# Last sequence's two experts: both first weights gathered before the second ones, the exp table loaded later, the second expert's part added to the sum from PSUM

## The chip, the cores and the metric

The kernel runs on one core of one Trainium2 chip. The metric is device microseconds (us) of one execution of the whole program. Engines are named as in the profile: PE does matrix products (PEld is its weight load), DVE is the vector engine, ACT the scalar engine with its function tables, POOL issues the indirect transfers, SP issues the plain ones. DVE and ACT read the matrix products out of PSUM, the accumulator memory[...]; everything else lies in SBUF.

## The reference, cut to what matters

Eight sequences of 1024 tokens with 256 channels pass a state-space layer (its recurrence over the tokens is the long part) with a feed-forward block, then attention with 8 heads, then a mixture of experts. The router looks at one sequence's mean, so all tokens of a sequence take the same two of the eight experts. In the reference this last part is

```python
logits = jnp.mean(x, axis=1) @ Wr + br                 # per sequence
...
top_w, top_i = jax.lax.top_k(rw_tok, K)                # K = 2
top_w = jax.nn.softmax(top_w, axis=-1)
h = jax.nn.gelu(jnp.einsum('nd,edf->enf', xf, W1) + b1[:, None, :], approximate=False)
y = jnp.einsum('enf,efd->end', h, W2) + b2[:, None, :]
out = jnp.einsum('ne,end->nd', w_dense, y).reshape(B, S, D)
out = _layer_norm(out + x, gamma, beta)
...
t = t + _L1_ffn_ref(_ln_t(t), ...)
```

So for each expert k of a sequence there are a product with W1 (256 to 512), a Gelu, a product with W2 (512 to 256), a weight w_k, and the sum of both; then the input is added, a layernorm follows, and the residual is added. The kernel centers W2 beforehand (the scratch tensor eW2_d), so the sum already has mean zero and the last layernorm needs only the variance.

## The kernel before, in words

Channels lie on partitions (256 channels are KC = 2 groups of 128), tokens along the free dimension, in chunks of CH = 512. A sequence is two chunks, c = 0 and 1. All data are fp32; the trace records two PE instructions for one fp32 product of 128 x 512.

The program is written as streams (Python generators: prologue, attention, experts, ...). Nothing schedules it afterwards: advance (L1808) walks a model clock, model.t, and lets each stream that is due emit its next instructions, the most urgent first. What a stream emits goes to the end of its engine's queue, and an engine takes its queue in order. A "yield" in a stream is a place where other streams may emit; "yield x" sets the model time from which the stream goes on. keep_warm (L1794) emits small products of 128 x 256 on zeros ("warm", or into a half bank under the name "halves") when the model sees PE free, so that PE stays busy.

All engine calls pass one helper, so nearly every instruction has the line L100 in the profile, and every transfer has L95; instructions are told apart by the names of what they write and read.

The part concerned is the end of the program. The last sequence (b = 7) has nothing after it, so it has its own path: experts (L1498) for b = B - 1 calls banks.widen(), which turns the two double PSUM banks that attention used into four single ones (named halves_0 and halves_1; names of tiles are shown without their numbers), so that six banks serve; then it starts two streams expert(b, 0, ...) and expert(b, 1, ...) (L1581) side by side. Each stream

- takes two SBUF tiles g1 and g2 and gathers its expert's weights by indirect DMA on the POOL queue: two gathers of 128 x 512 for W1 (L1587), at once followed by four of 128 x 256 for W2 (L1592). As the streams are started one after the other, the POOL queue holds g1, g2 of expert 0, then g1, g2 of expert 1;
- with k = 0 has weights() emit the small DVE work for the routing weights w2e and the two biases hbias and obias (L1482);
- for each chunk c: four products into PSUM (he, L1604), each taken out by ACT with a bias into the tiles he (names he<-halves,hbias and he<-he,hbias); two Gelus of 128 x 1024 on ACT (L1621); then lnexp() (L1623), which loads the table set with exp and ln; then two groups of four products (re, L1626), each taken out by ACT with weight w_k and bias into a tile r of this expert (L1634);
- when the second expert has its r for a chunk, finish_last (L1647) is started.

finish_last adds the two tiles r on DVE, adds the layernorm's input xf on DVE (two instructions of 128 x 1024), and runs layernorm (L387): ACT squares (sq_y), PE averages (16 short records), ACT does ln, exp and square on 128 x 128, DVE refines (two of 128 x 128), PE spreads the factors (pick), DVE scales, then adds beta and the residual t (four of 128 x 512), and SP writes the chunk out.

After both chunks, DVE forms a flag (L1950 to L1954), all engines load it and branch (L1957, L1960), and the program ends.

Of the kernel before, what the change touches and what calls it, by code (L numbers as in the profile page):

```python
# [12 lines left out]
AF = mybir.ActivationFunctionType  # L13
ALU = mybir.AluOpType
# [7 lines left out]
NCH = L // CH  # L22
# [32 lines left out]
def hybrid_kernel(ctx: ExitStack, tc: tile.TileContext, a: dict, out: bass.AP):  # L55
# [6 lines left out]
    class Model:  # L62
# [3 lines left out]
        t = end = moved = 0.0  # L66
# [10 lines left out]
    model = Model()  # L77
# [43 lines left out]
    def lnexp():  # L121

        act.preload_act_table_set("natural_log_exp_and_others")
# [146 lines left out]
    POLL = -1.0  # L270
# [204 lines left out]
    ends = {}  # L475
# [1022 lines left out]
    def experts(b: int):  # L1498

        rows1, rows2, w2e, hbias, obias, weights = yield from route(b)  # L1500
        if b == B - 1:

            banks.widen()
            parts = [[] for _ in range(NCH)]
            for k in range(2):
                start(
                    expert(b, k, rows1, rows2, w2e, hbias, obias, weights, parts), ("x", b, k),
                    model.t,
                )
            return  # L1510
        mem = Owner(t4, 5, 0)
        y_d = dram.tile([NCH, P, KC, CH], F32, name=f"y_d_{b}", tag="y_d", bufs=2)
        for k in range(2):
            g1 = yield from mem.take(f"g1_{b}_{k}")
            g2 = yield from mem.take(f"g2_{b}_{k}")
            g2v = g2.rearrange("p a (b n) -> p (a b) n", n=C)
            for i in range(KC):
                got = pool.indirect_dma_start(
                    out=g1[:, i, :], out_offset=None, in_=a["eW1"],
                    in_offset=bass.IndirectOffsetOnAxis(ap=rows1[:, k, i : i + 1], axis=0),  # L1520
                )
            for i in range(NF):
                pool.indirect_dma_start(
                    out=g2v[:, i, :], out_offset=None, in_=eW2_d,
                    in_offset=bass.IndirectOffsetOnAxis(ap=rows2[:, k, i : i + 1], axis=0),
                )
            if k == 0:
                yield
                weights()
            for c in range(NCH):  # L1530
                n = f"{b}_{k}_{c}"
                xf = yield from mem.take(f"xe_{n}")
                yield max(sp.dma_start(xf, xf_d[b][c]), got)
                hs, ps = [], None
                for f in range(NF + 1):
                    if f:
                        act.activation(
                            hs[(f - 1) // 2][:, 1 - f % 2, :], ps, AF.Identity,
                            bias=hbias[:, k, f - 1 : f],
                        )  # L1540
                        banks.put(ps)
                    if f < NF:
                        if f % 2 == 0:
                            hs.append((yield from mem.take(f"he_{n}_{f // 2}")))
                        ps = yield from banks.take(f"he_{n}_{f}")
                        for i in range(KC):
                            pe.matmul(
                                ps, g1[:, i, f * P : (f + 1) * P], xf[:, i, :],
                                start=(i == 0), stop=(i == KC - 1),
                            )  # L1550
                        yield
                mem.put(xf)
                for t in hs:
                    act.activation(t, t, AF.Gelu)
                lnexp()
                yield
                r = yield from mem.take(f"re_{n}")
                for m in range(KC):
                    ps = yield from banks.take(f"re_{n}_{m}")
                    for f in range(NF):  # L1560
                        pe.matmul(
                            ps, g2v[:, f, m * P : (m + 1) * P], hs[f // 2][:, f % 2, :],
                            start=(f == 0), stop=(f == NF - 1),
                        )
                    yield
                    act.activation(
                        r[:, m, :], ps, AF.Identity, bias=obias[:, k, m : m + 1],
                        scale=w2e[:, k : k + 1],
                    )
                    banks.put(ps)  # L1570
                yield
                mem.put(*hs)
                if k == 0:
                    mem.put(r, at=sp.dma_start(y_d[c], r))
                else:
                    mem.held -= 1
                    start(finish(b, c, r, y_d[c]), ("y", b, c), model.t)
            mem.put(g1, g2)
        mem.end()

    def expert(b: int, k: int, rows1, rows2, w2e, hbias, obias, weights, parts):  # L1581

        mem = Owner(t4, 5, 2)
        g1 = yield from mem.take(f"g1_{b}_{k}")
        g2 = yield from mem.take(f"g2_{b}_{k}")
        g2v = g2.rearrange("p a (b n) -> p (a b) n", n=C)
        for i in range(KC):  # L1587
            got = pool.indirect_dma_start(
                out=g1[:, i, :], out_offset=None, in_=a["eW1"],
                in_offset=bass.IndirectOffsetOnAxis(ap=rows1[:, k, i : i + 1], axis=0),  # L1590
            )
        for i in range(NF):  # L1592
            pool.indirect_dma_start(
                out=g2v[:, i, :], out_offset=None, in_=eW2_d,
                in_offset=bass.IndirectOffsetOnAxis(ap=rows2[:, k, i : i + 1], axis=0),
            )
        if k == 0:
            weights()
        yield got
        for c in range(NCH):  # L1600
            n = f"{b}_{k}_{c}"
            xf = ends[c][1]
            hs, ps = [], None
            for f in range(NF + 1):  # L1604
                if f:
                    act.activation(
                        hs[(f - 1) // 2][:, 1 - f % 2, :], ps, AF.Identity,
                        bias=hbias[:, k, f - 1 : f],
                    )
                    banks.put(ps)  # L1610
                if f < NF:
                    if f % 2 == 0:
                        hs.append((yield from mem.take(f"he_{n}_{f // 2}")))
                    ps = yield from banks.take(f"he_{n}_{f}")
                    for i in range(KC):
                        pe.matmul(
                            ps, g1[:, i, f * P : (f + 1) * P], xf[:, i, :],
                            start=(i == 0), stop=(i == KC - 1),
                        )
                    yield  # L1620
            for t in hs:  # L1621
                act.activation(t, t, AF.Gelu)
            lnexp()  # L1623
            yield
            r = yield from mem.take(f"re_{n}")
            for m in range(KC):  # L1626
                ps = yield from banks.take(f"re_{n}_{m}")
                for f in range(NF):
                    pe.matmul(
                        ps, g2v[:, f, m * P : (m + 1) * P], hs[f // 2][:, f % 2, :],  # L1630
                        start=(f == 0), stop=(f == NF - 1),
                    )
                yield
                act.activation(  # L1634
                    r[:, m, :], ps, AF.Identity, bias=obias[:, k, m : m + 1],
                    scale=w2e[:, k : k + 1],
                )
                banks.put(ps)
            yield
            mem.put(*hs)  # L1640
            parts[c].append(r)
            if len(parts[c]) == 2:
                start(finish_last(b, c, *parts[c], *ends[c]), ("y", b, c), model.t)
        mem.put(g1, g2)
        mem.end()

    def finish_last(b, c, r, r2, t, xf):  # L1647

        mem = Owner(t4, 4, 0, 4)
        vec.tensor_tensor(r, r, r2, ALU.add)  # L1650
        vec.tensor_tensor(r, r, xf, ALU.add)
        yield
        mem.put(r2, xf)
        yield from layernorm(mem, banks, r, r, f"y{b}_{c}", V("gamma"), centered=True)
        for m in range(KC):
            vec.scalar_tensor_tensor(
                r[:, m, :], r[:, m, :], V("beta", m), t[:, m, :], ALU.add, ALU.add
            )
        yield
        mem.put(t)  # L1660
        yield sp.dma_start(out_v[b, :, :, c * CH : (c + 1) * CH], r)
        mem.put(r)
        mem.end()
# [96 lines left out]
    with tc.tile_pool(name="work", bufs=1) as work_pool:  # L1760
# [30 lines left out]
        def start(stream, key, at=0.0):  # L1791
            due.append([at, URGENT[key[0]], len(done) + len(due), stream, key])
# [421 lines left out]
```

## Time and profile before

| what | us |
|---|---|
| median of 3 runs (lowest, highest) | 3543.58 (3540.22, 3544.69) |
| the profiled execution's own time | 3547.76 |
| its span, first to last instruction | 3546.0 |
| PE busy in the span | 3223.6 (91%) |
| DVE busy | 3070.7 (87%) |
| ACT busy | 2474.0 (70%) |
| first of the twelve gathers for b = 7 starts | 3443.71 |
| first product of the two experts starts | 3447.08 |
| last product of the two experts ends | 3522.88 |
| last chunk's store is issued | 3533.89 |

The profile gives for each instruction its start and duration in us from the start of the span, and in brackets how long its engine was idle before it and what ended that wait. An "x8" merges eight records of one kind that follow each other. In the records, ends of products are modelled: each overlaps the next by about 0.16 us. The stretch that the change touches is the last 100 us of a span of 3546 us. A wait for several semaphores is put down to the one that came last.

### The profile page before, as it was taken

To read this page: it belongs to the slowest core of one execution; us is meant where nothing else is said; L and a number is where in the kernel's file an instruction comes from. 1 tells how busy PE (TensorE), PEld (TensorE's weight loads), DVE (VectorE), ACT (ScalarE), POOL (GpSimd) and SP (SyncE) were. 2 spreads that over 40 slices of the span, in tenths; PEclk is the share of its full clock that TensorE was granted. 3 is DMA by queue.
4 is the path that set the end of the run, shared out by engine and by line. 5 is a ranking of instruction groups with operands and counts; after the bars stand their busy time and mean duration, and the time that the engine had idled before them with its cause. 6 is when DMAs were issued, how large, how long until landed. Compare 5 with 4: busy or idle time off the path is not lost. (4 is left out here: it accounts for less than half of the span.)

```text
span 3546.0 us, 39995 instructions
## 1 busy us (share of the span) xinstructions
PE 3223.6 (91%) x14425; PEld 1404.5 (40%) x14425; DVE 3070.7 (87%) x3160; ACT 2474.0 (70%) x3562; POOL 932.8 (26%) x1058
## 2 busy tenths in 40 slices
PE   8767878998999998989999999999999989999997
PEld 5454344333433344333433334333433343334344
DVE  6979999999999898999999899989998999942561
ACT  5643737785878776787778777886778777863644
POOL 0232223222331223323322233223422323211010
PEclk9878989999999999999999999999999999999999
DMA  4767888787888878898788988789888877842120
GB/s 124 191 133 162 193 184 187 171 199 181 196 204 186 187 182 191 187 202 200 181 195 191 201 188 192 180 188 215 197 203 191 196 174 183 211 110 72 36 75 16
DMA packets 189504, 607.79 MB, mean 171 GB/s; under 512 B 27056, under 2 KB 38000, under 8 KB 189296
## 3 DMA queue, kind: packets, MB, share of 16 engines
q0 software_dynamic: 103968, 366.54, 53.2%
q1 hardware_dynamic: 85328, 238.60, 20.9%
q8 instruction: 115, 1.88, 0.2%
q14 instruction: 93, 0.76, 0.1%
HBM read 238.58 MB, written 62.39 MB: 85 GB/s over the span
## 5 line engine op out<-in xcount | busy, mean ns | idle before, releaser
L100 ACT ACTIVATE da_all<-dt,vecs 128x512 f32<-128x512 f32 (+1 forms) x1024 | 702.3, 719 | 429.4 <-DVE hb L100 426.6
L95 POOL DMA_DIRECT2D dx<-hb x512 | 444.4, 870 | 1680.4 <-DVE hb L100 1334.3
L100 DVE TENSOR_TENSOR hb<-hb,bc 128x1024 f32<-128x1024 f32 x512 | 624.5, 1220 | 36.5 <-POOL state L100 26.6
L100 DVE TENSOR_TENSOR_SCAN hb<-da_all,state,hb 128x512 f32<-128x512 f32 x512 | 631.3, 1268 | 5.6 <-ACT da_all L100 5.6
L100 DVE TENSOR_TENSOR hb<-xm,bc 128x1024 f32<-128x1024 f32 x512 | 618.6, 1208 | 14.8 <-DMA dx<-hb 14.8
L100 DVE TENSOR_TENSOR_SCAN hb<-da_all,hb 128x1024 f32<-128x1024 f32 x256 | 584.5, 2283 | 3.7 <-ACT da_all L100 3.7
L100 ACT ACTIVATE pt<-sc 128x1024 f32<-128x1024 f32 x512 | 494.7, 1018 | 95.8 <-PE sc L100 80.5
L100 PE MATMUL warm<-mean_c,zero_c 128*128 128x256 f32 x1390 | 412.1, 425 | 43.0 <-ACT dt L100 11.4
L100 PEld LDWEIGHTS warm<-mean_c,zero_c 128*128 128x128 f32 x1390 | 261.6, 204 | 206.3 <-PE warm L100 82.5
L100 PE MATMUL sc<-qk,qk 32*128 32x512 f32 x2048 | 328.3, 645 | 14.7 <-ACT pt L100 8.9
L100 PE MATMUL num<-pt,v 128*32 128x512 f32 x2048 | 281.9, 621 | 49.7 <-DVE ot L100 49.7
L100 POOL COPY state<-hb 128x2 f32<-128x2 f32 x256 | 198.6, 776 | 363.3 <-DVE hb L100 347.8
L100 PE MATMUL den<-pt,ecb 128*32 128x512 f32 x1792 | 245.4, 618 | 0.0
L100 PE MATMUL facc<-fh,w 128*128 128x512 f32 x512 | 233.6, 601 | 7.3 <-ACT dt L100 2.2
L100 PE MATMUL fh<-x_f,w 128*128 128x512 f32 x480 | 229.1, 605 | 3.6 <-ACT xm L100 2.1
L100 PE MATMUL re<-he,g 128*128 128x512 f32 x472 | 216.4, 602 | 3.7 <-DVE xn L100 1.9
L100 ACT ACT_TABLE_LOAD x168 | 215.5, 1283 | 3.5 <-PEq L2201 0.7
L100 PE MATMUL he<-xe,g 128*128 128x512 f32 x448 | 217.5, 610 | 0.3 <-DVE x_f L100 0.2
L100 PEld LDWEIGHTS sc<-qk,qk 32*128 32x128 f32 x2048 | 96.3, 184 | 186.0 <-ACT pt L100 62.1
L100 PEld LDWEIGHTS facc<-fh,w 128*128 128x128 f32 x512 | 95.1, 191 | 132.6 <-issue 118.9
L100 PE MATMUL mo<-sz,w_out 128*128 128x512 f32 x256 | 124.7, 632 | 23.3 <-DVE sz L100 22.2
L100 PEld LDWEIGHTS num<-pt,v 128*32 128x32 f32 x2048 | 41.2, 108 | 245.4 <-issue 209.2
(364 smaller groups left out, 4331.0 us busy)
## 6 DMA issues: line engine op xcount, KB each, us to landing
dx<-hb POOLq DMA_DIRECT2D x512, 512.0 KB
bc<-bc_d SPq DMA_DIRECT2D x256, 512.0 KB
dt<-e POOLq DMA_DIRECT2D x38, 512.0 KB
dt<-u POOLq DMA_DIRECT2D x30, 512.0 KB
xe<-xf_d SPq DMA_DIRECT2D x28, 512.0 KB
xn<-in_x SPq DMA_DIRECT2D x16, 512.0 KB
xn_d<-xn SPq DMA_DIRECT2D x16, 512.0 KB
xz<-xn_d SPq DMA_DIRECT2D x16, 512.0 KB
```

Of the source, the lines that this page charges most:

```text
L95: f(*args, **kw)
L100: return f(*args, **kw)
```

## The change

Four edits in expert and finish_last, and one in experts; everything that is emitted before the twelve gathers is instruction for instruction the same.

- Between the g1 gathers and the g2 gathers a stream now yields, so both streams emit g1 first.
- lnexp() moves out of expert (after each pair of Gelus) to the start of finish_last (once for each chunk).
- The expert that comes first to a chunk takes its part out with ACT as before, now with the sum of both biases (one more small DVE addition in weights), and DVE adds xf to it at once. The other expert's part isn't taken out by ACT: DVE reads it from PSUM, multiplies by w_k and adds it to the first tile, one scalar_tensor_tensor of 128 x 512 for each of the two channel groups.
- finish_last has one tile less to add and none of the two additions.

```diff
@@ experts
-            parts = [[] for _ in range(NCH)]
+            parts = {}
@@ expert
         mem = Owner(t4, 5, 2)
+        begun = 0
...
                 out=g1[:, i, :], out_offset=None, in_=a["eW1"],
                 in_offset=bass.IndirectOffsetOnAxis(ap=rows1[:, k, i : i + 1], axis=0),
             )
+
+        yield model.t
         for i in range(NF):
             pool.indirect_dma_start(
                 out=g2v[:, i, :], out_offset=None, in_=eW2_d,
...
         if k == 0:
             weights()
+            vec.tensor_tensor(obias[:, 0], obias[:, 0], obias[:, 1], ALU.add)
         yield got
...
             for t in hs:
                 act.activation(t, t, AF.Gelu)
-            lnexp()
-            yield
-            r = yield from mem.take(f"re_{n}")
+            yield
+            one = c not in parts
+            if one:
+                parts[c] = None
+                begun += 1
+                r = yield from mem.take(f"re_{n}")
             for m in range(KC):
...
-                act.activation(
-                    r[:, m, :], ps, AF.Identity, bias=obias[:, k, m : m + 1],
-                    scale=w2e[:, k : k + 1],
-                )
+                if one:
+
+                    act.activation(
+                        r[:, m, :], ps, AF.Identity, bias=obias[:, 0, m : m + 1],
+                        scale=w2e[:, k : k + 1],
+                    )
+                else:
+                    while parts[c] is None:
+                        yield POLL
+                    r = parts[c]
+                    vec.scalar_tensor_tensor(
+                        r[:, m, :], ps, w2e[:, k : k + 1], r[:, m, :], ALU.mult, ALU.add
+                    )
                 banks.put(ps)
             yield
             mem.put(*hs)
-            parts[c].append(r)
-            if len(parts[c]) == 2:
-                start(finish_last(b, c, *parts[c], *ends[c]), ("y", b, c), model.t)
+            if one:
+                vec.tensor_tensor(r, r, xf, ALU.add)
+                parts[c] = r
+            else:
+                start(finish_last(b, c, r, *ends[c]), ("y", b, c), model.t)
         mem.put(g1, g2)
+        mem.gives = begun
         mem.end()
@@ finish_last
-    def finish_last(b, c, r, r2, t, xf):
-
-        mem = Owner(t4, 4, 0, 4)
-        vec.tensor_tensor(r, r, r2, ALU.add)
-        vec.tensor_tensor(r, r, xf, ALU.add)
-        yield
-        mem.put(r2, xf)
+    def finish_last(b, c, r, t, xf):
+
+        mem = Owner(t4, 4, 0, 3)
+        mem.put(xf)
+        lnexp()
         yield from layernorm(mem, banks, r, r, f"y{b}_{c}", V("gamma"), centered=True)
```

## The prediction

> **What bounds the kernel now.** I read the page first: PE is busy 91% of the span, and the change leaves everything before the twelve gathers at 3443.71 as it was. So only the last 100 us count. The view by windows shows that PE is not full there and that no other engine is either:
>
> ```profile
> 3450.00:3500.00 50.00, 43.44 (x110) 18.68 (x108) 2.45 (x2) 23.15 (x28) 6.62 (x7) 0.93 0.09 27
> 3500.00:3546.00 46.00, 30.85 (x117) 18.35 (x116) 9.60 (x18) 15.52 (x21) 0.00 (x0) 0.91 0.07 25
> ```
>
> Columns: length, busy us of PE, PEld, DVE, ACT and POOL, granted PE clock, DMA share, GB/s. Next, PE's timeline of that stretch, for its three pauses:
>
> ```profile
> 3449.50 1.88 PE L100 MATMUL he<-xf,g 128*128 128x512 f32 x4
> 3454.88 3.29 PE L100 MATMUL he<-xf,g 128*128 128x512 f32 x4 [3.50 <-DMA g<-in_eW,rows]
> ...
> 3465.39 1.88 PE L100 MATMUL he<-xf,g 128*128 128x512 f32 x4
> ...
> 3471.64 5.40 PE L100 MATMUL halves<-he,g 128*128 128x512 f32 x8 [3.06 <-ACT he L100]
> ...
> 3503.99 3.40 PE L100 MATMUL halves<-xf,g 128*128 128x512 f32 x4 [3.87 <-ACT sq_y L100]
> ```
>
> Each pause costs twice. Four records normally take 1.88 (1.72 when the next follows at once) and eight 3.43; after the pauses they take 3.29, 5.40 and 3.40. The clock in 4 us windows falls to 0.62, 0.59 and 0.64 there: 1.5 to 2.0 us lost after each.
>
> The first pause waits for expert 1's W1. POOL's timeline tells why; the two gathers of g from in_eW for expert 1 stand behind four from eW_d:
>
> ```profile
> 3443.71 1.07 POOL L95 DMA_INDIRECT g<-in_eW,rows  x1 [32.52 <-DVE rows L100]
> 3445.08 1.00 POOL L95 DMA_INDIRECT g<-in_eW,rows  x1 [0.30 <-issue]
> 3446.39 0.95 POOL L95 DMA_INDIRECT g<-eW_d,rows  x1 [0.30 <-DVE obias L100]
> 3447.64 0.95 POOL L95 DMA_INDIRECT g<-eW_d,rows  x1 [0.30 <-issue]
> ...
> 3451.39 0.95 POOL L95 DMA_INDIRECT g<-in_eW,rows  x1 [0.30 <-issue]
> ```
>
> The second waits for a PSUM bank whose eviction (3470.89) stands on ACT behind two table loads and two Gelus:
>
> ```profile
> 3466.30 1.28 ACT L100 ACT_TABLE_LOAD   x1
> 3467.59 2.00 ACT L100 ACTIVATE he<-he 128x1024 f32<-128x1024 f32 x2
> 3469.60 1.28 ACT L100 ACT_TABLE_LOAD   x1
> 3470.89 0.69 ACT L100 ACTIVATE he<-halves,hbias 128x512 f32<-128x512 f32 x1
> ```
>
> The third is alike, for chunk 1. Last, the chain that ended last, at the point where the products end: one eviction and two DVE additions stand before the square.
>
> ```profile
> 3519.45 3.45 PE re L100 x8
> 3522.92 0.79 ACT re L100
> 3523.73 1.24 DVE re L100
> 3524.99 1.24 DVE re L100
> 3526.31 1.07 ACT sq_y L100
> ```
>
> **What the skill says.** (1) The Trainium skill, ScalarE: Activation LUTs, What ACT_TABLE_LOAD costs: about 1283 ns, plus a drain of some 1380 ns. The trace agrees with the load (1.28) and shows no such drain: the eviction at 3465.59 takes 0.69, the load starts at 3466.30. I price a load at 1.28. (2) Same page, Table sets: cheap functions such as identity are in every set. So an eviction (Identity with bias) between Gelus needs no load; the trace has no such order yet, but the changed program, built, has four loads where the old one has eight, none at an eviction. (3) TensorE: Matmul & The Clock Gate, Part 1: PE falls to half its clock after an idle window of about 3.4 us and stays there about as long. The trace agrees: pauses of 3.06 to 3.87 double the records' times, those of 1.21 and 1.49 near the same place don't; elsewhere 1.83 (577.76) and 2.17 (751.47) do, 1.91 (1849.28) and 2.49 (477.69) don't. (4) VectorE: DVE Perf Modes, Why PSUM operands drop a tier: fp32 with PSUM runs at the base rate. DVE's rows agree that this is no loss: re<-re,vecs,halves, which reads PSUM, takes 1.41 for two, as re<-re,vecs,x1l from SBUF does.
>
> **The change, stage by stage.** I put the changed program's instructions, in their built order and with their built waits, one behind the other: each starts when its engine is free and what it waits for has ended, with the durations above (0.03 from one engine to another). The old order walked in this way, with 1.8 added after each pause over 2.5, ends 0.5 before the trace; that is the method's error.
>
> A, first layer of chunk 0 (old: 3447.08 to 3467.27). Expert 1's two W1 gathers take the POOL places at 3446.39 and 3447.64. From start to product a gather takes 3.37 to 3.49 (3443.71 to 3447.08; 3451.39 to 3454.88), so they land at 3449.8 and 3451.1. The second half of the second group ends at 3452.0; six groups of 1.72 follow: end 3462.3 with the overlap. Gain 5.0: the pause and its slow records. The W2 gathers lose 2.50 (expert 0) and nothing (expert 1); expert 0's land by 3456.1, needed at 3464: covered by 8 us of products. If gathers in flight together land one POOL place later, this loses 1.25; the low end is 0, since they can't land before their issue.
>
> B, to the first product of the second layer (old: 4.37 later, 3471.64). It waits for one Gelu only, and its bank isn't the one evicted late: last evictions end 3461.9, load 1.28, Gelu 1.01: 3464.1. PE idles 1.0. Gain 2.5.
>
> C, to the last product ahead of the third pause (old: 28.49, to 3500.13). PE is full: four re groups 3.43, seven he groups 1.72, variance 0.57, one warm 0.43, overlap 0.16: 26.9. Gain 1.6, the slow records. The new DVE work (1.24 and two of 0.71) and ACT's exp load, square and evictions lie beside it. The square waits for DVE until 3480.8; behind it on ACT stand evictions whose banks PE asks for after 3483, and he groups that wait for DVE itself to free a bank have 6 us to spare. The added sum of biases (0.17, like the row of 128 x 16) ends 3 us before the first eviction.
>
> D, to the last product (old: 22.75, to 3522.88). Here a wait appears. ACT's ln for chunk 0 waits for a PE count that, in the built order, a later product group brings; behind it stand the Gelus. PE in turn waits for the factors: ln, exp, square 1.04, DVE 0.62, handovers: 1.75 idle. Then pick 0.89, one he 1.72, four re 13.72, warm 0.43, 0.16: 18.7. Gain 4.1: 3.87 of pause become 1.75, 1.5 of slow records and one warm go. Cover is thin: the Gelus are ready 0.3 to 1.3 ahead of PE.
>
> E, to the store (old: 11.01). The last part takes one DVE instruction of 0.71 (bounds 0.66, the shortest row of its size, and 0.79, ACT's eviction) instead of 0.79 + 1.24 + 1.24; adding xf, 1.24, is hidden beside the last group of 3.43 (if not, +1.24), and so is the exp load, 1.28, on ACT. But five warm products stand in PE's queue ahead of the variance, one waiting for that DVE read: 2.15 against 1.06 for the square, and one more ahead of pick: +1.5. So 9.5. Gain 1.5.
>
> Sum: 5.0 + 2.5 + 1.6 + 4.1 + 1.5 = 14.7; less the method's error 14.3. The store moves to about 3519.4. After it (12.1 us to the span's end) all is as before, but PE loads the flag 0.6 after DVE made it, behind its warm products; in the new order fewer follow: 0 to 0.6 more. I take 14.6. The profiled execution, 3547.76 with span 3546.0 (1.76 around it), would become 3533.2, span 3531.4. It was 4.2 above the median of the runs; the gain, a difference, comes off the median: 3543.58 - 14.6 = 3529.0.
>
> **Rivals.** (1) PE's slow clock remains: the idle times of 1.0 and 1.75 and the wait for gathers are in the range where the trace shows both. One to two times 1.8: 3530.8 to 3532.6. For: 1.83 sufficed once. Against: 1.91 once not. (2) The gain is smaller because covers fail: gathers land a place later (1.25), Gelus come late for PE in D (up to 2), xf isn't hidden (1.24): 4.5 less, 3533.5. (3) The change doesn't do what it says on ACT: evictions between Gelus need tables after all. From the built order, Gelu then eviction then Gelu occurs twice and evictions follow Gelus twice, so six loads of 1.28: 7.7 less, 3536.7, no change by measurement. Against: no load is in the program. (4) Slower: without its pauses PE is throttled for longer. Place: PE from 3447 to the end, some 60 us of products. Price: at half clock a product takes twice its time, so each us of work so treated costs one. It turns slower from 14.6 us so treated, by over 0.2% from 21.7; with 25, 3554. Against: from 3250 to 3300 PE is busy 50.00 of 50.00 at clock 1.00.
>
> **Numbers.** Likeliest case 0.68 (its own range 3526 to 3532), rival 1 0.15, rival 2 0.07, rival 3 0.07, rival 4 0.03. The range 3525.0 to 3534.5 takes in the first three with their bounds (runs of before spread by 4.5) and leaves out rivals 3 and 4 and the tails. A measurement tells 0.2%, 7.1 us, from no change: faster by more 0.90 (cases 1 to 3), within 0.07 (rival 3), slower 0.03 (rival 4).
>
> **What would show it.** After: gathers of in_eW four in a row on POOL; no PE pause of over 2 us between 3447 and the last re product, and no clock window of 0.6; four table loads after 3443 instead of eight; the first re product near 3464; PE idle some 1.8 ahead of pick, after an ln that waits; DVE's re<-halves,w2e,re at 0.7; the store near 3519.4. Wrong if a pause with doubled records remains, if ACT shows loads at evictions, or if anything before 3443 moves by several us.

## The result, and the profile after

The changed kernel takes 3525.77 us (median of 4 runs, 3520.60 to 3532.03) against 3542.61 (4 runs, 3540.22 to 3544.69): ratio 0.9953, interval 0.9936 to 0.9971. Measured again on another chip it takes 3525.89 (9 runs) against 3541.33 (24 runs): 0.9962, interval 0.9949 to 0.9975. The prediction was 3529.0, with a range from 3525.0 to 3534.5.

The first profile of the changed kernel is of a run of 3532.03, the slowest of the four, with a span of 3530.1: 15.9 less than the 3546.0 before. The gathers start at 3439.07 and the last store is issued at 3517.63. From the first gather to the store is therefore 78.56 us, where the kernel before had 3443.71 to 3533.89, 90.18. This length, "the tail" below, is 11.62 shorter. The start of the gathers moved by 4.64, after instructions that are the same in both kernels, and the stretch after the store takes 0.36 more (12.47 for 12.11).

The view by windows of the changed kernel, with the columns shown before:

```profile
3450.00:3500.00 50.00, 47.01 (x129) 21.57 (x128) 6.04 (x9) 23.56 (x31) 3.04 (x4) 0.97 0.07 22
3500.00:3530.00 30.00, 19.59 (x88) 12.64 (x86) 6.57 (x13) 4.88 (x7) 0.00 (x0) 0.90 0.06 21
```

PE is busy 47.01 of 50 (43.44 before) at a granted clock of 0.97 (0.93 before). PE's timeline shows where it still waits:

```profile
3445.46 3.99 PE L100 MATMUL he<-xf,g 128*128 128x512 f32 x8 [0.47 <-DMA g<-in_eW,rows]
...
3456.15 1.88 PE L100 MATMUL he<-xf,g 128*128 128x512 f32 x4
...
3460.04 10.57 PE L100 MATMUL halves<-he,g 128*128 128x512 f32 x24 [1.14 <-ACT he L100]
...
3485.38 1.88 PE L100 MATMUL halves<-xf,g 128*128 128x512 f32 x4
3489.11 1.68 PE L100 MATMUL halves<-sq_y,pick 128*128 128x128 f32 x8 [1.85 <-DVE sq_y L100]
3490.58 3.08 PE L100 MATMUL he<-xf,g 128*128 128x512 f32 x4
...
3504.23 3.59 PE L100 MATMUL halves<-he,g 128*128 128x512 f32 x8
```

The three pauses of 3.06 to 3.87 are gone. The pause of 1.85 ahead of pick is new, and slow records follow it: 1.68 for pick, whose eight records otherwise take 1.05 (1.16 right after a wait), and 3.08 for four he records that otherwise take 1.88. Between 3490 and 3494 the granted clock of PE is 0.63. POOL's timeline has the four gathers from in_eW in a row:

```profile
3439.07 1.07 POOL L95 DMA_INDIRECT g<-in_eW,rows  x1 [32.50 <-DVE rows L100]
3440.44 1.00 POOL L95 DMA_INDIRECT g<-in_eW,rows  x1 [0.30 <-issue]
3441.75 0.95 POOL L95 DMA_INDIRECT g<-in_eW,rows  x1 [0.30 <-issue]
3443.00 0.95 POOL L95 DMA_INDIRECT g<-in_eW,rows  x1 [0.30 <-issue]
```

ACT's timeline loads a table four times in the tail where it loaded eight times before. An eviction between Gelus has no load of its own (3460.84), and the ln of chunk 0 (eps_t) waits 3.00:

```profile
3457.63 1.28 ACT L100 ACT_TABLE_LOAD   x1
3458.93 2.00 ACT L100 ACTIVATE he<-he 128x1024 f32<-128x1024 f32 x2
3460.84 0.67 ACT L100 ACTIVATE he<-he,hbias 128x512 f32<-128x512 f32 x1
3461.41 1.99 ACT L100 ACTIVATE he<-he 128x1024 f32<-128x1024 f32 x2
...
3487.36 0.37 ACT L100 ACTIVATE sq_y<-halves,eps_t 128x128 f32<-128x128 f32 x1 [3.00 <-PE halves L100]
```

### The profile page after: what moved, and what is told of

Same layout as the page of the kernel before. It is cut to its first block, busy times and chain, and to the rows that moved or that the text cites. A ratio compares the mean times of both kernels' runs of the same rounds, so it can differ in the third digit from the quotient of the medians.

```text
span 3530.1 us, 39986 instructions
## 1 busy us (share of the span) xinstructions
PE 3225.6 (91%) x14423; PEld 1404.9 (40%) x14423; DVE 3072.1 (87%) x3163; ACT 2462.2 (70%) x3554; POOL 936.5 (27%) x1058
## 3 DMA queue, kind: packets, MB, share of 16 engines
q8 instruction: 115, 1.88, 0.2%
## 5 line engine op out<-in xcount | busy, mean ns | idle before, releaser
L100 DVE TENSOR_TENSOR hb<-xm,bc 128x1024 f32<-128x1024 f32 x512 | 619.4, 1210 | 14.7 <-DMA dx<-hb 14.6
```

The costliest lines, as they stand in the source:

```text
L100: return f(*args, **kw)
```

## The experiments

Three questions were open. Does each part bring its own share, or do the parts remove the same pauses? Is the pause of 1.85 the cause of the slow records, and what causes the pause? And has the change anything to do with the 4.64 us ahead of the gathers?

All kernels were timed beside the kernel before on the same chip. "Tail" is from the start of the first gather to the issue of the last store, in the one profiled run of each row.

| kernel | us | before, same chip | ratio, interval | gathers start | tail |
|---|---|---|---|---|---|
| changed, first pair | 3525.77 | 3542.61 | 0.9953 (0.9936 to 0.9971) | 3439.07 | 78.56 |
| changed again | 3525.89 | 3541.33 | 0.9962 (0.9949 to 0.9975) | 3438.20 | 76.90 |
| before again, one run | 3545.23 | 3546.98 | - | 3441.55 | 89.69 |
| gather order alone | 3536.53 | 3547.00 | 0.9973 (0.9964 to 0.9982) | 3444.66 | 78.85 |
| table loads alone | 3539.14 | 3547.00 | 0.9978 (0.9969 to 0.9988) | 3445.84 | 80.03 |
| PSUM sum alone | 3538.80 | 3547.00 | 0.9980 (0.9973 to 0.9987) | 3445.49 | 82.52 |
| all but gather order | 3537.61 | 3546.98 | 0.9972 (0.9962 to 0.9981) | 3438.43 | 79.72 |
| all but table loads | 3536.61 | 3546.98 | 0.9973 (0.9961 to 0.9986) | 3448.49 | 81.39 |
| all but PSUM sum | 3533.64 | 3541.33 | 0.9981 (0.9972 to 0.9990) | 3431.67 | 79.93 |
| changed, pause filled | 3533.40 | 3547.00 | 0.9966 (0.9957 to 0.9976) | 3438.71 | 76.91 |
| own bank | 3529.11 | 3541.33 | 0.9966 (0.9956 to 0.9976) | 3434.97 | 74.52 |
| own bank, not warm | 3524.04 | 3541.33 | 0.9959 (0.9946 to 0.9972) | 3433.98 | 73.62 |
| the same, again | 3529.91 | 3546.98 | 0.9953 (0.9938 to 0.9969) | 3441.33 | 75.24 |

The times say less than the tails: the 53 runs of the kernel before in one row of measurements lie between 3539.95 and 3554.85, while its two profiles differ by 0.5 in the tail.

**One part alone.** The gather order:

```diff
+        yield model.t
         for i in range(NF):
             pool.indirect_dma_start(
```

> The kernel before with one part of the change alone: both experts' first weights are gathered before the second ones. Measure: the length from the start of the first of the twelve gathers to the issue of the last store, 90.18 us in the profile of before and 78.56 in that of after. Theory 'the parts overlap' (the old built order, with this one edit, walked through with the old durations): once PE no longer pauses in the first layer, the order that follows also has its later evictions, Gelus and banks in time, so that this edit alone brings 12.4: length 77.7, no pause of over 2.5 us on PE, or 79.5 if one short pause triggers slow records. Rival 'the parts add up' (each stage of the prediction belongs to one part): only stage A is gained, 5.0: length 85.2, and the later pauses of about 3.06 and 3.87 with doubled records stay. Rival 'the gather order is all of it': as long as after, 78.6, and the other two parts alone do nothing. In time: 12 below before, or 5 below.

The table loads:

```diff
@@ expert
-            lnexp()
@@ finish_last
+        lnexp()
         yield from layernorm(
```

> The kernel before with one part of the change alone: the exp table is no longer loaded after each pair of Gelus but once for each chunk, in the last step. Theory 'the parts overlap': the pause at the gathers of 3.5 with its slow records stays, the two later ones go: gain 10.9, length from the first gather to the store 79.2. Rival 'the parts add up': stages B, C and D of the prediction, 8.2: length 82.0. Rival 'the gather order is all of it': length 90, as before.

The sum from PSUM: the rest of the change's diff, without these two edits.

> The kernel before with one part of the change alone: the second expert's part is added straight from PSUM, the layernorm's input is added to the first part at once, the two whole additions at the end are gone. The gather order and the table loads are as before. Theory 'the parts overlap': the pause at the gathers stays, and one more with slow records; gain 8.2, length from the first gather to the store 81.8. Rival 'the parts add up': only stage E, 1.5: length 88.7. Rival 'the gather order is all of it': length 90, as before.

Measured: the tail falls by 11.33, 10.15 and 7.66. The theory of overlap gave 12.4 (10.7 with one slow stretch), 10.9 and 8.2. Adding up gave 5.0, 8.2 and 1.5. The three alone come to 29.1, all together to 11.6 and 13.3. So the parts remove the same pauses, and the timelines show which. The third pause of the kernel before (3.87, at 3503.99) waits for the ln of chunk 0, which stands on ACT behind two loads and two Gelus:

```profile
3502.27 1.28 ACT L100 ACT_TABLE_LOAD   x1
3503.57 0.37 ACT L100 ACTIVATE sq_y<-halves,eps_t 128x128 f32<-128x128 f32 x1
```

Each of the three parts alone removes it; at most 1.29 is left, with the gather order. The second (3.06) goes with the gather order and with the table loads (1.43 is left), but stays with the sum. The first goes with the gather order only. In PE's timeline with the table loads alone it is still there:

```profile
3457.04 3.35 PE L100 MATMUL he<-xf,g 128*128 128x512 f32 x4 [3.42 <-DMA g<-in_eW,rows]
```

With the sum alone PE is already slow ahead of it (2.83 for four he records), so 1.53 of it is left; the second pause costs more than before (6.64 for the eight records, 5.40 before):

```profile
3472.04 6.64 PE L100 MATMUL halves<-he,g 128*128 128x512 f32 x8 [3.06 <-ACT he L100]
```

How does the gather order alone remove a pause that was put down to table loads? By ACT's timeline of that kernel it still loads eight times, and an eviction still stands behind two loads and two Gelus:

```profile
3463.33 1.28 ACT L100 ACT_TABLE_LOAD   x1
3464.63 2.00 ACT L100 ACTIVATE he<-he 128x1024 f32<-128x1024 f32 x2
3466.65 1.28 ACT L100 ACT_TABLE_LOAD   x1
3467.94 0.69 ACT L100 ACTIVATE he<-he,hbias 128x512 f32<-128x512 f32 x1
```

But PE doesn't wait for it. PE's timeline of the same kernel has no idle time ahead of its first group of the second layer:

```profile
3465.74 3.69 PE L100 MATMUL re<-he,g 128*128 128x512 f32 x8
3469.27 7.03 PE L100 MATMUL halves<-he,g 128*128 128x512 f32 x16
```

In the kernel before, the late eviction empties a half of a double bank (he<-halves), and PE's next group goes to the double banks: PE waits 3.06. Here the late eviction empties a single bank (he<-he), PE's next group goes to another bank (re), and it starts between the loads, 2.2 before the eviction. The evictions that empty the double banks all stand ahead of the loads in this kernel. So the order of the groups, of the banks and of ACT's queue is another one; that it is another because expert 1's groups were emitted earlier is likely, but not shown by itself.

**One part undone.** The same three edits taken back from the changed kernel, one at a time.

> The changed kernel with the first part undone: each expert's second weights are gathered right behind its first ones again; table loads and sum as changed. Theory 'the parts overlap': only the pause at the gathers comes back, with slow records; walked through with the old durations (plus 0.9, see above) the length from the first gather to the store is 79.3, 2.4 more than the 76.90 of the changed kernel's second profile, though the same edit alone brought 11.3. Rival 'each part's worth is its own': 11 is lost, length 88.

> The changed kernel with the second part undone: the exp table is loaded after each pair of Gelus as before; gather order and sum as changed. Theory 'the parts overlap': one long pause of PE comes back late, near the first re product of chunk 1 (4.4 in the walk), with slow records: length 80.0, 3.1 more than 76.90, though the same edit alone brought 10.2. Rival 'each part's worth is its own': 10 is lost, length 87.

> The changed kernel with the third part undone: gather order and table loads as changed, but both parts taken out of PSUM by ACT and two whole DVE additions in the last step, as before. Theory 'the parts overlap, PE's own work is the floor': only the end after the last product is lost, and hardly a pause comes back; length from the first gather to the store 78.4 (walked through with the old durations, plus the 0.9 by which the changed kernel's profile exceeded such a walk), 80.2 if a short pause triggers slow records. Rival 'the parts add up': what the third part brought alone, 7.7, is lost: length 84 to 86.

Measured: 79.72, 81.39 and 79.93, within 1.4 of the theory of overlap and far from the rival's 84 to 88. This is 2.8, 4.5 and 3.0 more than the 76.90 of the changed kernel's second profile. With the other two in place each part is worth a quarter to under a half of what it is worth alone, and in these profiles 1.4 to 2.6 of that is slow records, of which the profile they are compared with has none. Without the table move one long pause comes back, where the walk had it; PE's timeline shows slow records after it (9.73 for sixteen instead of 7.03):

```profile
3507.19 9.73 PE L100 MATMUL halves<-he,g 128*128 128x512 f32 x16 [4.41 <-ACT re L100]
```

**The pause ahead of pick.** First PE was kept busy in it, with products of zero weights that nothing reads:

```diff
+        if name == f"y{B - 1}_0":
+            idle_ps = psum.tile([P, CH], F32, name="fill", tag="num")
+            for _ in range(4):
+                pe.matmul(
+                    idle_ps[:, : CH // 2], zero_w, mean_c.to_broadcast([P, CH // 2]),
+                    start=True, stop=True,
+                )
         for q in range(4):
             pe.matmul(
                 ps[:, q * P : q * P + P], pick[:, q : q + 1].to_broadcast([P, P]), r,
```

> The changed kernel with four products of zero weights (128 x 256 each, into a bank that nothing uses) that PE runs while it waits for chunk 0's factors, where the profile of after shows 1.85 us of idle time ahead of pick and then slow records (pick 1.68 instead of 1.05, four he products 3.08 instead of 1.88). Theory 'the short pause triggers the slow clock': with PE busy in it the records keep their 1.05 and 1.88 and the length from the first gather to the store falls from 78.56 by 1.8 to 76.7. Rival 'the slow records come from something else, such as the load just before': they stay, and the length stays near 78.6. If the products are longer than the pause, up to 1.0 is lost again.

Then the changed kernel was run again as it is:

> The changed kernel again, unchanged, for a second profile and more runs. Two questions. First: in the first pair of profiles the gathers start 4.64 us earlier in the changed kernel although every instruction before them is the same, and the median fell by 16.8 where the tail explains 11.6. Theory 'the body only spreads': the start of the gathers lies anywhere between 3438 and 3446, as in the profiles of the three kernels with one part each (3444.66, 3445.84, 3445.49), and the time falls by 12 to 14 against the kernel before on the same chip. Rival 'the change makes the body faster': the gathers start near 3439 again and the time falls by 16 to 17. Second: the pause of 1.85 us ahead of pick. Theory 'a pause of this length triggers the slow clock sometimes': pick and the four he products behind it take either 1.05 and 1.88 (length from the first gather to the store 76.7) or 1.7 and 3.1 again (78.6).

With the filling the records are normal (pick 1.16, he 1.88) and the tail is 76.91. That looks like the proof, but the changed kernel's second profile has the same pause of 1.85, and normal records too, with a tail of 76.90:

```profile
3488.26 1.16 PE L100 MATMUL halves<-sq_y,pick 128*128 128x128 f32 x8 [1.85 <-DVE sq_y L100]
3489.25 1.88 PE L100 MATMUL he<-xf,g 128*128 128x512 f32 x4
```

So the filling alone shows nothing. What the two profiles of one program show is that slow records follow this pause in some executions and not in others, and that they are the whole of the 1.66 between 78.56 and 76.90 (from the product group ahead of the pause to the last expert product: 20.56 and 18.89). In the second profile the granted clock of PE stays at 1.00 there (3488 to 3496).

Next, the pause itself. Chunk 0's variance is one half of a double bank; later products go to the other half. Here the last two layernorms got a bank of their own:

```diff
-        ps = yield from bank.take(f"var_{name}")
+        last = name.startswith(f"y{B - 1}_")
+        if last:
+            ps = psum.tile([P, CH], F32, name=f"var_{name}", tag="num")
+        else:
+            ps = yield from bank.take(f"var_{name}")
...
-        bank.put(ps)
+        if not last:
+            bank.put(ps)
```

> The changed kernel, but the variance and the factors of the last two layernorms get a PSUM bank of their own (one that the attention before has given back) instead of half of a shared double bank. Theory 'ln waits because the two halves of the shared bank count as one': ln then follows the variance at once (its wait of 3.00 on PE falls under 0.5), PE has no pause ahead of pick, all of PE's products from the first of the second layer to the last follow each other, and the length from the first gather to the store is 74.5 against 78.56 (1.9 of slow records and 2.1 of pause and order less); in time 4 below the changed kernel, or 2 if that one has no slow records in most runs. Rival 'ln is late for another reason, such as ACT's own queue': the wait stays, the length stays at 77 to 78.6.

The ln now follows the variance without a wait, behind one eviction. ACT's timeline of this kernel:

```profile
3479.10 1.26 ACT L100 ACTIVATE he<-halves,hbias 128x512 f32<-128x512 f32 x2 [2.75 <-PE halves L100]
3480.25 0.37 ACT L100 ACTIVATE sq_y<-var_y,eps_t 128x128 f32<-128x128 f32 x1
```

And PE's: from variance to pick it has no pause.

```profile
3478.99 0.64 PE L100 MATMUL var_y<-sq_y,mean_c 128*32 128x128 f32 x16
3479.56 1.99 PE L100 MATMUL halves<-xf,g 128*128 128x512 f32 x4
3481.38 1.88 PE L100 MATMUL he<-xf,g 128*128 128x512 f32 x4
3483.10 1.05 PE L100 MATMUL var_y<-sq_y,pick 128*128 128x128 f32 x8
```

The tail is 74.52, as expected; so the sharing of the double bank was the cause of the wait. In time no gain is seen: 3529.11, where 2 to 4 below the changed kernel was expected and that one took 3525.89 on the same chip, with the runs of both spread by 9 or more. (The planner also emits the groups behind the factors in another order here; variance, ln and pick stand as before, with two groups of four between variance and pick.) The Trainium skill, PSUM — Partial Sum Buffer, PSUM bank collisions raise a hardware error, advises to guard PSUM by bank and quadrant; by the bank size that its Specifications state, 512 fp32 values, the two halves are two banks. The program seems to guard the whole tile, so that the wait was wider than that advice asks for. The run agrees: with the banks apart it is gone. (The trace gives the tiles without their numbers, so it doesn't name the two halves.)

Last, the warm products behind the last expert product were left out (no part of the output):

```diff
+    ended = []
...
                 start(finish_last(b, c, r, *ends[c]), ("y", b, c), model.t)
+                ended.append(c)
...
-            if pe.at > model.t - 0.2:
+            if pe.at > model.t - 0.2 or len(ended) == NCH:
                 return
```

> As the kernel with a bank of its own for the last variances, and also without the warm products after the last expert product. Theory of the prediction's stage E 'warm products stand in PE's queue ahead of variance and pick': from the last expert product to the store 1.0 less (8.8 instead of 9.8), so length 73.5, and PE loads the flag up to 0.6 sooner after DVE made it. Rival 'the warm products keep the clock up': variance and pick come after pauses of 1.8 and take twice as long, 1.0 for pick, and nothing is gained or 0.8 is lost: length 74.5 to 75.3.

> The kernel with a bank of its own for the last variances and without the warm products after the last expert product, unchanged, for a closer time. Its tail was 73.62 in the first profile, 16.6 less than before's 90.18, and its time 17.3 below before. Theory 'the tail is all of the difference': 16 to 18 below before again, length 73.6 within 0.5. Rival 'the first time was a chance of the body's spread': 12 to 14 below before.

From the last product to the store: 9.45 with them; 8.41 without them in the first profile, 9.33 in the second. Each of the two theories about the warm products was right once. The pauses that the warm products filled are there both times; slow records follow them the second time. (The second tail was expected within 0.5 of 73.6 and is 75.24; the time still fell by 17.1, after 17.3.) PE's timeline of the first profile:

```profile
3501.13 0.64 PE L100 MATMUL var_y<-sq_y,mean_c 128*32 128x128 f32 x16 [1.50 <-ACT sq_y L100]
3503.65 1.16 PE L100 MATMUL var_y<-sq_y,pick 128*128 128x128 f32 x8 [1.88 <-DVE sq_y L100]
```

And of the second, with the same waits and 2.08 for pick:

```profile
3509.17 0.64 PE L100 MATMUL var_y<-sq_y,mean_c 128*32 128x128 f32 x16 [1.50 <-ACT sq_y L100]
3511.70 2.08 PE L100 MATMUL var_y<-sq_y,pick 128*128 128x128 f32 x8 [1.88 <-DVE sq_y L100]
```

The first profile of this kernel has the shortest tail of all; its two tails are 1.7 to 4.9 shorter than those of the changed kernel, but the second is longer than the 74.52 with the warm products. In time the two can't be told apart: 0.9959 and 0.9953 against 0.9962 and 0.9953, with wide intervals.

**The stretch ahead of the gathers.** The kernel before ran again for a second profile:

> The kernel before again, unchanged, for a second profile. Theory 'the body only spreads': the length from the first gather to the store is 90.2 within 0.5 (the pauses of 3.5, 3.06 and 3.87 with their slow records come in every execution), while the start of the gathers differs from 3443.71 by up to 8 us either way. Rival 'the tail spreads as well': the length differs by 2 or more.

Its tail is 89.69, within 0.5 as expected, though slow records follow two of its three pauses and not all. Its gathers start at 3441.55. Over all profiles this start lies between 3431.67 and 3448.49, and not by the parts that a kernel has: the earliest lacks the PSUM sum, the latest lacks the table move. Nine of the fourteen profiles have a wait of 2.38 to 4.00 us in PE at the same instruction, between 3223 and 3233, put down to "remote"; five have not, the changed kernel's two among them. The first profile of the kernel before has it. PE's timeline there:

```profile
3226.01 0.70 PE L100 MATMUL warm<-mean_c,zero_c 128*128 128x256 f32 x2
3229.20 0.70 PE L100 MATMUL warm<-mean_c,zero_c 128*128 128x256 f32 x2 [2.49 <-remote]
...
3231.64 1.92 PE L100 MATMUL var_t<-sq_t,pick 128*128 128x128 f32 x8
...
3234.01 1.88 PE L100 MATMUL he<-xe,g 128*128 128x512 f32 x4
```

And of the changed kernel's first profile:

```profile
3226.02 2.22 PE L100 MATMUL warm<-mean_c,zero_c 128*128 128x256 f32 x6
3228.07 1.05 PE L100 MATMUL var_t<-sq_t,pick 128*128 128x128 f32 x8
...
3229.40 1.88 PE L100 MATMUL he<-xe,g 128*128 128x512 f32 x4
```

Up to 3226 the two are level to 0.01; at the he products, behind the stop and its slow records, they are 4.61 apart, and at the gathers 4.64. So this stop is the whole of the 4.64. In all nine profiles it moves what follows by 3.9 to 7.6, against the profiles without it. It isn't the program: the kernel without warm products has it in one profile (2.53) and not in the other. All four profiles from one chip were without it, all eight from two others had it, and on those two the kernel before took 5.7 longer (3547.00 and 3546.98 against 3541.33). From which chip the first two profiles come, and which of the timed runs had the stop, is not on record.

In times the rival that the change makes the body faster is not settled as clearly. When the changed kernel ran again, its gathers started at 3438.20 and the time fell by 15.4, between the 12 to 14 of the theory and the 16 to 17 of the rival; but it had no stop either. Where the time fell by more than the tail (16.8 for 11.6, 15.4 for 13.3), it fell by less in other kernels (7.7 for 10.3 in all but the PSUM sum, 12.2 for 15.7 with a bank of its own). Over the twelve comparisons of the table what the time fell by less what the tail fell by is 0.2 on average, between -3.4 and +5.2. The interval of the first ratio alone reaches from 10.3 to 22.7 us, so the tail's 11.6 lies in it. That the changed kernel keeps a small part of its 5.2 and 2.2 can't be excluded.

## Why the prediction was right, point by point

The time lay 3.2 below the forecast, inside the range. The mechanism was right: what PE waits for came as forecast in every stage. That the time lay so near is in part luck. Two errors stand against each other: the tail gained 11.6 and 13.3 instead of 14.6, and the time of the first pair fell by 5.2 more than its tail, which nothing had forecast. It is the same with the store, forecast near 3519.4 and issued at 3517.63: the tail was some 3 longer, but it began 4.64 earlier, because the stop was missing. Two of the forecast's own signs of being wrong came up in the first profile. Something before 3443 moved by several us; that was the stop and not the change. And a pause with slow records remained (1.85, clock 0.63); that was the mechanism of rival 1, and in the second profile the records were normal. Against the forecast lengths, by stage (A to the last product of chunk 0's first layer, B to the first product of the second layer, C to the pause ahead of pick, D to the last expert product, E to the store):

| stage | forecast | first profile | second profile |
|---|---|---|---|
| first gather to first product | 3.37 | 3.42 | 3.28 |
| A | 15.2 | 15.54 | 15.70 |
| B | 1.87 | 2.01 | 2.00 |
| C | 26.9 | 27.22 | 27.23 |
| D | 18.7 | 20.56 | 18.89 |
| E | 9.5 | 9.81 | 9.80 |

- A: right in kind. Expert 1's gathers, with others in flight, feed PE 3.6 to 3.7 after their start (3441.75 and 3443.00 to 3445.46 and 3446.60) instead of 3.37 to 3.49, so PE waits 0.47 ahead of its first group. The bound of 1.25 held, its low end 0 did not.
- B and C: right to 0.14 and 0.33. The Gelu and no eviction is what PE waits for (1.14). C's extra is in steps of 0.1 at each change from one kind of product to another (1.98 for four after the variance).
- D: the pause came as forecast, 1.85 for 1.75, with the ln that waits. The term "1.5 of slow records" was counted as gained whole. The first profile paid 1.7 of slow records again, the second none. This is rival 1; it is a chance in each execution and not one case or the other, so the forecast should have taken part of it into the sum.
- E: DVE's new instruction took 0.75 for 0.71; the addition of xf (1.23) and the exp load lay beside PE's last group, as forecast. But the terms as written don't add to 9.5: 11.01 less 2.56 for the shorter chain, plus 1.5 for the warm products ahead of variance and pick, is 9.95, and 9.81 and 9.80 were measured. Without the 1.5 the sum is 8.45, and the kernel without warm products took 8.41 in the profile in which the clock stayed up. (As printed, two other sums are off by 0.1: 14.7 less the method's 0.5 is 14.2, not 14.3, and the terms of B give 3464.2, not 3464.1.)
- After the store: wrong in sign. Up to 0.6 more gain was forecast, because PE would load the flag sooner. PE does load it sooner (together with the other engines at 3518.3, 0.6 behind them before), but the stretch got 0.36 and 0.19 longer. What takes the time there stays open.
- Rival 2 had the right kind for one cover (gathers, 0.3 to 0.5 instead of 1.25); Gelus and xf were covered. Rival 3 is refuted: four loads, none at an eviction. Rival 4: PE is at clock 1.00 in the windows around 3480, and no profile shows a lasting throttle.

What the prediction did not see is the overlap. It named one cause for each pause, and each cause was real in the old order; but the three parts were worth 11.3, 10.2 and 7.7 alone, and 2.8 to 4.5 as the last one added. The sum over stages of the whole change came near (14.6 for 11.6 and 13.3) because it was taken from the changed program's own order, not from prices of the edits.

## What to carry to other kernels

A pause belongs to an order of instructions and banks, not to one cause: when a planner deals buffers anew, one early edit can remove the later pauses too, so walk the whole new order through instead of adding up the prices of edits, and expect the second and third edit to be worth far less. An instruction such as a table load costs what another engine waits for it, which may be nothing. When the stretch that a change touches is a few per cent of the span, compare that stretch's length in the profiles, several of each, before believing a difference of times. And where two profiles differ in a stretch that is the same in both programs, line them up at a common instruction and look where they part.

## What was not expected of the hardware

- Slow records after a pause of PE are a matter of chance over a wide range of lengths. Of ten pauses of 3.06 to 4.41 us in these tails nine were followed by records that took 1.4 to 2.9 longer together, and one (3.06, second profile of the kernel before) by none, although the same pause cost 1.7 in the first profile. Of five of 1.85 to 1.88, two were, with 1.7 and 0.9, and a third only after the next pause, of 1.13, with 1.4. The waits of about 1.2 and 0.2 to 0.5 for the first gathers, which all fourteen profiles have, were followed by them in two. The Trainium skill, TensorE: Matmul & The Clock Gate, Part 1, says that the clock's window of activity is free-running, so that the change of speed depends on where in the window the work falls. The two outcomes of one program agree with that; the pauses of 1.85 are shorter than the idle window of about 3.4 us that it states, so for the loss after them the measurement decides.
- The stop of 2.4 to 4.0 us in PE at one instruction, in all profiles from two chips and in none from another, moves the rest by 3.9 to 7.6 us, and nothing in the program tells of it. Its cause stays open.
